# A three-layer CIN on one core: four first-half chunks instead of five ahead of the second layer's weights, and seven shared groups instead of six

## The chip, the core and the metric

The kernel runs on one core of one Trainium2 chip. The metric is the device time of one execution in microseconds; lower is better. Before the change it is 500.84 us, the median of three runs (500.74 to 501.07). The profiled execution has a span of 499.2 us; all times of the profile below are counted from the start of that span.

## The reference

A batch of 1024 samples has 64 fields of 16 values each. Three layers of "compressed interaction" follow one another, and the sums of their outputs give one number for each sample:

```python
x0 = h = x                                   # (1024, 64, 16), float32
for i in range(3):                           # W0, W1, W2: 128 outputs each
    z = einsum('bfe,bge->bfge', x0, h)       # all products of a field of x with a row of h
    y = einsum('oc,bce->boe', W[i], z.reshape(B, -1, E)) + b[i]
    x_i, h = (y[:, :64], y[:, 64:]) if i < 2 else (y, y)
    xs.append(x_i)
pooled = concatenate(xs, axis=1).sum(axis=2)
return pooled @ fc_w.T + fc_b
```

Every weight beyond the first layer's lower half enters the output linearly, so the kernel folds them together. With `fc` for the matching part of `fc_w`:

- `h1` is the first layer's lower half: 64 outputs, each a quadratic form of x.
- V2 is W2 summed over its outputs with `fc`: a 64 x 64 matrix. M is W1's lower half summed with V2: M[f1, f2, g] = sum over o of V2[f1, o] W1[64 + o, f2, g]. So M too gives 64 quadratic forms of x, and the third layer is the sum over g of h1[g] times M's form g, plus small terms.
- V1 and V0 are the upper halves of W1 and W0 summed with `fc`: V1 is linear in x and is added to M's form, V0 is one quadratic form of x.

So each sample needs 128 quadratic forms of x, 64 from W0 and 64 from M, and M has to be computed first, from W2 and W1.

## The kernel before

The batch is cut into 32 chunks of 32 samples, so a chunk has 512 columns (32 samples x 16 values). Of each chunk the products of two fields are made by VectorE: 16 tiles of 128 products x 512 columns, in four instructions of four tiles each (`product(c, j)`, j = 0 to 3, line 166), from two copies of x that are shifted against one another (`xa`, `xb`, 1 MB each). ScalarE puts the 32 squares that fit into the last group (line 171). The squares left over make a 17th, smaller tile (`last_tile`).

TensorE contracts these tiles with `w_all`, whose columns 0 to 63 are W0's, 64 to 127 M's and 128 to 191 W0's again. All is float32, so each matmul is two instructions in the profile. There are three ways to do a chunk:

- As two halves, `half_contract(c, part, j)`, line 237: part 0 is h1 and needs W0 alone, part 1 is M's and needs M. The 512 columns are split over the two halves of the array's columns. `keep_h1` (line 243) saves part 0's result in `hb`.
- Whole, `contract(c, j)`, line 198, 128 outputs at once, with a 17th tile of its own (`contract_last`, line 205).
- Whole, with a shared 17th tile: four chunks' squares lie one below another in one tile, and `contract_shared` (lines 207 to 224) does the four in one go, with V1's and V0's matmuls (`acc` and `y`) of all four chunks. Only chunks from `FIRST` on do this.

M is not there at the start. So the kernel first does part 0 of five chunks, `HEAD = [4, 5, 6, 0, 1]`, called c0 to c4, and puts the work on M between them. In TensorE's order: c0; V2's two sums over W2 (line 307); two groups of c1; V2's transposition (line 324); one more group of c1; M's matmuls (line 336); the rest of c1; c2; c3; three groups of c4. M is written to DRAM (six transfers, lines 357 to 363, onto a square that is extended on two sides) and read back skewed (lines 393 to 406: two transfers, then eight `ms` reads of 256-byte pieces, then `dg` and `w_sq`), and VectorE adds the two orders of fields into `w_all` (line 415). The reads wait for all writes. The last two heads, chunks 0 and 1 (`KEPT`), keep their products, so their part 1 follows as soon as M is there. The other three heads, 4, 5 and 6, have their products made again later, for part 1. The loop over the remaining work goes `order = 2, 3, 4, ..., 31` and makes the products of the chunk two places ahead.

What sets the order: it is written out by hand. Each engine runs its instructions in the order of the program, and a tile of a pool waits until the readers of the tile that had its place are done. There are 12 places for products (`z`), 3 for `xa` and for `xb`, and in PSUM 4 for `acc`, 2 for `y` and 2 for `set`. In the loop `v0x(k)` (line 267) computes V0's form for the pair of chunks 2k and 2k + 1 into a `y` tile, and `x_v0x(k)` (line 270) reads that tile on VectorE; `contract_shared` writes two `y` tiles as well. `factors(c)` (lines 257 and 263) multiplies the two halves of a chunk, and `sums` (line 274) sums them over the 16 values.

The sums of W1 and W0 with `fc` (`weigh`, lines 436 and 437) go to VectorE between the products of the first chunks behind M.

Of the kernel before, what the change touches and what calls it, by code (L numbers as in the profile page):

```python
# [44 lines left out]
N = CB * E  # L45
# [3 lines left out]
NT = NI * NJ  # L49
XR = 128 + NI  # L50
EXT = 96
HEAD = [4, 5, 6, 0, 1]
NF = len(HEAD)
KEPT = HEAD[-2:]
NV = 200
FIRST = 8
SQ = slice(96, 128)


# [1 line left out]
def cin_kernel(ctx, tc, xra, xrb, xh, wh, w0r, w1h, w2t, wx1, wx0, vec, out):  # L61
# [51 lines left out]
    nc.gpsimd.memset(bd, 0.0)  # L113


    xas, xbs, zls, xxs = {}, {}, {}, {}

    def load_xa(c, at=slice(0, NI)):
        if c not in xas or at.start == 0:
# [12 lines left out]
        nc.sync.dma_start(out=xb, in_=xrb[c])  # L132
        xbs[c] = [xb[:, j, :] for j in range(NJ)]

    c0, c1, c2, c3, c4 = HEAD
    xb0 = z_tile("xb0")
    w0t = z_tile("w0t")
    w2s = [flat_tile(f"w2_{k}") for k in range(2)]
# [9 lines left out]
    load_chunk(c1)  # L148
    for k in range(2):
        nc.sync.dma_start(out=w2s[k], in_=w2t[k])  # L150
    load_chunk(c2)
    nc.sync.dma_start(out=w1s, in_=w1h)


    acc = const_tile("acc", [128, 2, NCH // 2, CB])
# [3 lines left out]
    def new_acc(c, n=N):  # L159
        accs[c] = ps.tile([128, n], F32, tag="acc", name=f"acc_{c}", bufs=4)  # L160

    def product(c, j, pieces=1):
        zs[c, j] = z_tile(f"z_{c}_{j}")
        n = NI // pieces
        for i in range(0, NI, n):
            nc.vector.tensor_tensor(  # L166
                zs[c, j][:, i : i + n, :], xas[c][:, i : i + n, :],
                xbs[c][j].unsqueeze(1).to_broadcast([128, n, N]), ALU.mult,
            )
        if j == NJ - 1:  # L170
            nc.scalar.activation(zs[c, j][SQ, 0, :], xas[c][SQ, 0, :], AF.Square)  # L171

# [4 lines left out]
    def last_tile(c):  # L177

        if c < FIRST:
            squares(c)  # L180
            nc.scalar.copy(zls[c][64:128], xas[c][64:128, 0, :])  # L181
        else:
            if c % 4 == 0:
                zls[c // 4] = xp.tile([128, N], F32, tag="zl", name=f"sq_{c}", bufs=4)
            at = 32 * (c % 4)
            nc.scalar.activation(zls[c // 4][at : at + 32], xas[c][0:32, 0, :], AF.Square)  # L186
# [8 lines left out]
    def contract(c, j):  # L195
        for i in range(NI):
            t = j * NI + i
            nc.tensor.matmul(  # L198
                accs[c], w_all[:, t, w_cols(c)], zs[c, j][:, i, :],
                start=(t == 0 and (c < FIRST or c % 4 < 2)),  # L200
                stop=(t == NT - 1 and c >= FIRST and c % 4 >= 2),
            )

    def contract_last(c):
        nc.tensor.matmul(accs[c], w_all[:, NT, 0:128], zls[c], start=False, stop=True)  # L205

    def contract_shared(first):

        for r in range(4):
            c, at = first + r, slice(32 * r, 32 * r + 32)  # L210
            nc.tensor.matmul(  # L211
                accs[c], w_sq[at, w_cols(c)], zls[first // 4][at], start=(r >= 2), stop=(r < 2),
                tile_position=(32 * r, 0),
            )
# [35 lines left out]
    def factors(c):  # L250

        uu = uu_tile(c // 2)[halves[c % 2], 0, :]
        if c in HEAD:
            for n in range(2):
                at = halves[n]
                nc.vector.tensor_tensor(  # L256
                    uu[:, n * H2 : (n + 1) * H2], accs[c][at], hb[at, HEAD.index(c), :], ALU.mult
                )
            return
        h = halves[c % 2 if c >= FIRST else 0]  # L260
# [25 lines left out]

    new_acc(c0, H2)
    squares(c0)
    for j in range(NJ):
        product(c0, j, 2 if j == 0 else 1)  # L290
        if j == NJ - 1:
            nc.vector.memset(w0s[j][SQ, 0, 1, :], 0.0)
        h1_weights(j)
# [21 lines left out]
    new_acc(c1, H2)  # L315
    for j in range(NJ - 1):
        product(c1, j)
    for j in range(2):
        half_contract(c1, 0, j)
    pt = ps.tile([128, F // 4, 4], F32, tag="acc", name="pt", bufs=4)  # L320
    v2q = v2r.rearrange("p n (s o) -> p (n s) o", o=F)
    for q in range(F // 4):
# [1 line left out]
            nc.tensor.matmul(pt[to, q, :], v2q[:, q, :], pick, start=True, stop=True)  # L324
    nc.scalar.copy(v2t, pt.rearrange("p q k -> p (q k)"))
    product(c1, NJ - 1)
    half_contract(c1, 0, 2)
    load_chunk(c4)


    m_sb = z_tile("m_sb")
# [8 lines left out]
    for m in range(NI):  # L340
        nc.scalar.copy(m_sb[:, m, :], pms[m])  # L341

    for j in range(3, NJ + 1):
        half_contract(c1, 0, j)


# [27 lines left out]
    def head(c):  # L374
        new_acc(c, H2)
        for j in range(NJ):
            product(c, j)
        for j in range(NJ + 1):
            half_contract(c, 0, j)
        keep_h1(c)  # L380

    head(c2)

# [12 lines left out]
        )  # L396
    for i in range(NI):
        for half in range(2):
            queue = nc.scalar if half and i < 2 else nc.sync
            queue.dma_start(  # L400
                out=ms[halves[half], 1].rearrange("p (j i) g -> p j i g", i=NI)[:, :, i, :],
                in_=skewed(i, 16 * half + 4, [[4 * F, NJ], [1, F]]),
            )
# [11 lines left out]
    nc.vector.tensor_tensor(w_all[:, 0:NT, 64:128], ms[:, 0], ms[:, 1], ALU.add)  # L415
    nc.vector.tensor_copy(w_all[SQ, (NJ - 1) * NI, 64:128], dg[SQ])
    nc.vector.tensor_copy(w_all[0:32, NT, 64:128], w_sq[0:32, 64:128])
    product(c4, NJ - 1)
    load_chunk(2)
    w1x = flat_tile("w1x")  # L420
    nc.sync.dma_start(out=w1x, in_=wx1)
    new_acc(c3, H2)
    for j in range(NJ):
        half_contract(c3, 1, j)
    for j in range(NJ - 1, NJ + 1):
        half_contract(c4, 0, j)
    keep_h1(c4)
    new_acc(c4, H2)
    for j in range(NJ):
        half_contract(c4, 1, j)  # L430

    def weigh(w, fc, out):

# [3 lines left out]
        nc.vector.tensor_reduce(out, w, AX.X, ALU.add)  # L437


    last_tile(2)  # L440
    for j in range(NJ):
        product(2, j)
    v1h = const_tile("v1h", [128, 32])
    weigh(w1x, fcr[:, 64:128], v1h)
    for to in halves:
# [24 lines left out]
    nc.scalar.activation(cst, pc, AF.Identity, bias=fcb, scale=float(E))  # L470


    last_tile(3)
    for j in range(NJ):
        product(3, j)
    v0h = const_tile("v0h", [128, 32])
    weigh(w0x, fcr[:, 0:64], v0h)
    for to in halves:
# [17 lines left out]
        nc.scalar.dma_start(out=outs[:, pairs, :], in_=res[:, pairs, :])  # L496


    order = list(range(2, NCH))
    first, last = slice(0, NP - 1), slice(NP - 1, NP)  # L500
    for s, c in enumerate(order):
        k, shared = c // 2, c >= FIRST
# [6 lines left out]
        if not shared or c % 4 < 2:  # L509
            new_acc(c, H2 if c in HEAD else N)  # L510
        for j in range(NJ):
            if j == 2:
                if s == 0:
                    for n in KEPT:
                        half_contract(n, 1, NJ)
                if s == 1:
                    v0x(0)
                if c % 2 and not shared:
                    v0x(k)
                if s == len(order) - 1:  # L520
                    pool(first, 1)
                    pool(first, 0)
            if c in HEAD:
                half_contract(c, 1, j)
            else:
                contract(c, j)
        if c in HEAD:
# [23 lines left out]
        if c % 2 and not shared:  # L551
            x_v0x(k)
        elif s and c % 2 == 0:
            sums(k - 1)
    sums(NP - 1, parts=slice(1, 2))
    sums(NP - 1, slice(0, 64), slice(0, 1))
    pool(last, 1)
# [76 lines left out]
```

## Time and profile before

| engine | busy us | share of the span |
|---|---|---|
| TensorE matmuls (PE) | 483.8 | 97% |
| TensorE weight loads (PEld, beside the matmuls) | 222.6 | 45% |
| VectorE (DVE) | 381.8 | 76% |
| ScalarE (ACT) | 92.5 | 19% |

The transfers move 82.8 MB, 166 GB/s over the span, but in the first 40 us, while weights and first chunks arrive, some 420 GB/s. A line of the profile names the engine, the line of the kernel and the tiles (output <- inputs); a bracket at its end is the time in which the engine stood still before it, and what ended that. In a timeline the two numbers at the front are the start and the length in us. Of a wait for several things the profile names the last one by its reckoning.

Four moments of the span matter: the first matmul at 8.44 us, M's writes issued at 33.56, M's columns in `w_all` complete at 53.4, and the loop's first matmul at 72.57.

### The profile page before, as it was taken

What the parts mean: (1) busy time and instruction counts of PE and PEld (TensorE: products, weight loads), DVE (VectorE), ACT (ScalarE), POOL (GpSimd) and SP (SyncE); (2) the same over time, 40 slices, a digit from 0 to 9 for tenths busy, and PEclk for the clock granted to TensorE, in tenths of its full rate; (3) what the DMA queues carried; (4) which work ended last, traced back from release to release, by engine and by line L of the source; (5) the groups of instructions that cost most, each with busy time, mean ns of one, the idle gap of its engine ahead of it and who ended that gap; (6) DMA issues with size and microseconds to landing.
All of it is one profiled execution on the core that took longest, in us unless ns stands there. A gap on an engine that the chain in (4) does not pass through costs nothing.

```text
span 499.2 us, 4338 instructions
## 1 busy us (share of the span) xinstructions
PE 483.8 (97%) x1814; PEld 222.6 (45%) x1814; DVE 381.8 (76%) x233; ACT 92.5 (19%) x159; POOL 1.4 (0%) x14
## 2 busy tenths in 40 slices
PE   3899999999999999999999999999999999999996
PEld 1455654456444344443444434443444434444432
DVE  4999699988999889898777686776877777770302
ACT  1243033122111121312011121111111121010001
POOL 1000000000000000000000000000000000000000
PEclk9999999999999999999999999999999999999999
DMA  8997895353454443446144442333444430000000
GB/s 327 425 419 226 338 421 208 116 230 129 181 235 175 170 174 162 177 175 256 66 169 169 168 168 113 118 136 138 168 169 168 167 131 39 0 0 0 2 0 0
DMA packets 14787, 82.80 MB, mean 166 GB/s; under 512 B 3788, under 2 KB 4460, under 8 KB 5232
## 3 DMA queue, kind: packets, MB, share of 16 engines
q1 hardware_dynamic: 13644, 81.24, 41.5%
q10 hardware_dynamic: 1124, 1.29, 0.9%
q8 instruction: 14, 0.23, 0.2%
q14 instruction: 5, 0.04, 0.0%
HBM read 80.88 MB, written 1.64 MB: 165 GB/s over the span
## 4 chain that ended last, share of the span: by engine, by line
PE 91%; DMA 5%; ACT 1%; ACTq 0%; SPq 0%; DVE 0%; issue 0%
PE acc L198 75%; PE acc L237 11%; DMA w1s<-in_w1h 4%; PE acc L219 2%; DMA xb<-in_xrb 1%; PE acc L211 1%; PE y L267 1%; PE acc L205 1%; PE pm L336 0%; PE po L489 0%; ACT zl L175 0%; ACT zl L181 0%; ACT m_sb L341 0%; ACT xx L190 0%; ACTq L360 0%
## 5 line engine op out<-in xcount | busy, mean ns | idle before, releaser
L198 PE MATMUL acc<-z,w_all 128*128 128x512 f32 x864 | 374.1, 593 | 0.0
L166 DVE TENSOR_TENSOR z<-xa,xb 128x2048 f32<-128x2048 f32 (+1 forms) x141 | 314.9, 2270 | 49.9 <-PE acc L198 39.7
L198 PEld LDWEIGHTS acc<-z,w_all 128*128 128x128 f32 x864 | 163.3, 190 | 208.3 <-issue 207.8
L237 PE MATMUL acc<-z,w_all 128*64 128x256 f32 x640 | 74.7, 389 | 10.4 <-DVE w_all L282 8.4
L171 ACT ACTIVATE z<-xa 32x512 f32<-32x512 f32 x35 | 21.9, 625 | 323.5 <-DVE z L166 320.7
L263 DVE SCALAR_TENSOR_TENSOR uu<-acc,vs,q 64x512 f32<-64x512 f32 x27 | 20.2, 750 | 62.4 <-ACT q L262 62.3
L237 PEld LDWEIGHTS acc<-z,w_all 128*64 128x64 f32 x640 | 45.8, 140 | 39.1 <-DVE w_all L282 9.9
L274 DVE TENSOR_REDUCE acc<-uu 128x64 f32<-128x1024 f32 (+2 forms) x18 | 20.2, 1125 | 0.3
L190 ACT COPY xx<-xa 64x512 f32<-64x512 f32 x32 | 19.6, 613 | 0.4
L262 ACT COPY q<-acc 64x512 f32<-64x512 f32 x27 | 15.7, 580 | 19.3 <-PE y L224 12.9
L186 ACT ACTIVATE sq<-xa 32x512 f32<-32x512 f32 x24 | 15.1, 628 | 0.6
L270 DVE SCALAR_TENSOR_TENSOR uu<-y,cx,xx 128x512 f32<-128x512 f32 x16 | 11.4, 745 | 0.3
L224 PE MATMUL y<-xx,bd 64*64 64x512 f32 x48 | 11.6, 602 | 0.0
L219 PE MATMUL acc<-xx,v1w 64*64 64x512 f32 x48 | 11.6, 602 | 0.0
L211 PE MATMUL acc<-sq,w_sq 32*128 32x512 f32 x48 | 6.8, 640 | 0.0
L175 ACT ACTIVATE zl<-xa 64x512 f32<-64x512 f32 x11 | 6.8, 623 | 0.1
L219 PEld LDWEIGHTS acc<-xx,v1w 64*64 64x64 f32 x48 | 2.8, 132 | 7.9 <-issue 7.9
L237 PE MATMUL acc<-zl,w_all 64*64 64x256 f32 (+1 forms) x40 | 6.1, 393 | 0.0
L243 ACT ACTIVATE hb<-acc,vs 128x256 f32<-128x256 f32 x5 | 2.4, 474 | 20.0 <-PE acc L237 20.0
L495 ACT ACTIVATE res<-po,cst 2x480 f32<-2x480 f32 (+1 forms) x2 | 0.9, 464 | 24.0 <-PE po L489 24.0
L181 ACT COPY zl<-xa 64x512 f32<-64x512 f32 x8 | 4.9, 616 | 0.1
L256 DVE TENSOR_TENSOR uu<-acc,hb 64x256 f32<-64x256 f32 x10 | 4.2, 421 | 0.2
(52 smaller groups left out, 52.0 us busy)
## 6 DMA issues: line engine op xcount, KB each, us to landing
xa<-in_xra SPq DMA_DIRECT2D x34, 1024.0 KB, 4.8
xb<-in_xrb SPq DMA_DIRECT2D x34, 1024.0 KB, 7.0
w<-in_w2t SPq DMA_DIRECT2D x2, 1024.0 KB, 13.5
xa<-in_xra SPq DMA_DIRECT2D x2, 512.0 KB, 4.1
w1s<-in_w1h SPq DMA_DIRECT2D x1, 1024.0 KB, 20.3
w1x<-in_wx SPq DMA_DIRECT2D x1, 1024.0 KB, 8.7
w0x<-in_wx SPq DMA_DIRECT2D x1, 1024.0 KB, 10.3
xb<-in_xrb SPq DMA_DIRECT2D x1, 768.0 KB, 7.0
```

Source lines behind the costliest of these rows:

```text
L166: nc.vector.tensor_tensor(zs[c, j][:, i : i + n, :], xas[c][:, i : i + n, :], xbs[c][j].unsqueeze(1).to_broadcast([128, n, N]), ALU.mult,)
L171: nc.scalar.activation(zs[c, j][SQ, 0, :], xas[c][SQ, 0, :], AF.Square)
L186: nc.scalar.activation(zls[c // 4][at : at + 32], xas[c][0:32, 0, :], AF.Square)
L190: nc.scalar.copy(xxs[c // 2][to], xas[c][to, 0, :])
L198: nc.tensor.matmul(accs[c], w_all[:, t, w_cols(c)], zs[c, j][:, i, :], start=(t == 0 and (c < FIRST or c % 4 < 2)), stop=(t == NT - 1 and ...
L211: nc.tensor.matmul(accs[c], w_sq[at, w_cols(c)], zls[first // 4][at], start=(r >= 2), stop=(r < 2), tile_position=(32 * r, 0),)
L219: nc.tensor.matmul(accs[c][q], v1w[rows], xxs[k][rows], start=False, stop=(c % 4 < 2), skip_group_check=True,)
L224: nc.tensor.matmul(ys[k][rows], bd[rows, rows], xxs[k][rows], start=True, stop=True)
L237: nc.tensor.matmul(accs[c][halves[n]], w_all[rows, t, cols], z[rows, n * H2 : (n + 1) * H2], start=(t == 0), stop=(t == NT),)
L262: nc.scalar.copy(q[h], accs[c][64 - h.start : 128 - h.start])
L263: nc.vector.scalar_tensor_tensor(uu, accs[c][h], bh1[h], q[h], ALU.add, ALU.mult)
L274: nc.vector.tensor_reduce(acc[rows, parts, k, :], uus[k][rows, parts].rearrange("p k (b e) -> p k b e", e=E), AX.X, ALU.add,)
```

## The change

The change does one head fewer, and gives the chunks 4 to 7 to the cheaper shared way: the heads are the chunks 2, 3, 0 and 1, `FIRST` is 4, and the loop goes 4, 5, 6, 7, 2, 3, 8, ..., 31. With it go a new order of the first part and smaller edits:

- Twelve matmuls of zeros (`pw`) at the start, so that TensorE is active before its first data come.
- `w1s` (W1's half for M) is loaded ahead of chunk c2; the first chunk's last weight sum comes ahead of its last product.
- V2's transposition and M's matmuls each come one group of c1 earlier.
- The chunk `FIRST` = 4 is loaded ahead of M's writes, in the place where c4 was loaded, and nothing is loaded beside M's reads. One of M's eight skewed reads goes from SP's queue to ACT's, and `keep_h1(c2)` comes behind the reads.
- The sum that makes M's columns is cut in two, so that the first four tiles are ready sooner, and comes behind the first product of chunk 4. `w1x` takes the place of `ms`.
- In the loop `contract_last` falls away, and the places of `factors`, `v0x` and `sums` follow the new order.

```diff
-HEAD = [4, 5, 6, 0, 1]
+HEAD = [2, 3, 0, 1]
-FIRST = 8
+FIRST = 4
...
+    pw = ps.tile([128, 128], F32, tag="y", name="pw")
+    for k in range(12):
+        nc.tensor.matmul(pw, bd, bd, start=True, stop=True)
...
+    nc.sync.dma_start(out=w1s, in_=w1h)
     load_chunk(c2)
-    nc.sync.dma_start(out=w1s, in_=w1h)
...
+    h1_weights(2)
+    nc.vector.memset(w0s[3][SQ, 0, 1, :], 0.0)
+    h1_weights(3)
+    product(c0, 3)
...
-    for j in range(2):
-        half_contract(c1, 0, j)
+    half_contract(c1, 0, 0)
...
     product(c1, NJ - 1)
-    half_contract(c1, 0, 2)
-    load_chunk(c4)
+    half_contract(c1, 0, 1)
+    load_chunk(FIRST)
...
-    for j in range(3, NJ + 1):
+    for j in range(2, NJ + 1):
         half_contract(c1, 0, j)
...
-            queue = nc.scalar if half and i < 2 else nc.sync
+            queue = nc.scalar if half and i < NI - 1 else nc.sync
...
+    keep_h1(c2)
     head(c3)
-    new_acc(c4, H2)
-    for j in range(NJ - 1):
-        product(c4, j)
-        half_contract(c4, 0, j)
-    nc.vector.tensor_tensor(w_all[:, 0:NT, 64:128], ms[:, 0], ms[:, 1], ALU.add)
+    keep_h1(c3)
+    last_tile(FIRST)
+    product(FIRST, 0)
+    for at in (slice(0, NI), slice(NI, NT)):
+        nc.vector.tensor_tensor(w_all[:, at, 64:128], ms[:, 0, at], ms[:, 1, at], ALU.add)
...
-    product(c4, NJ - 1)
-    load_chunk(2)
-    w1x = flat_tile("w1x")
+    for j in range(1, NJ):
+        product(FIRST, j)
+    w1x = set_tile("w1x")
...
+    for c in KEPT:
+        new_acc(c, H2)
+        for j in range(NJ):
+            half_contract(c, 1, j)
...
-    load_chunk(3)
+    load_chunk(FIRST + 1)
...
-    order = list(range(2, NCH))
+    order = [4, 5, 6, 7, 2, 3] + list(range(8, NCH))
...
-        elif not shared:
-            contract_last(c)
         elif c % 4 == 1:
             for n in (1, 2):
                 new_acc(c + n)
             contract_shared(c - 1)
...
-        elif not shared or c % 4 in (0, 3):
+        elif head or c % 4 in (0, 3):
             factors(order[s - 1])
+            if order[s - 1] % 2:
+                sums(order[s - 1] // 2)
         elif c % 4 == 2:
             factors(c - 2)
             factors(c - 1)
             x_v0x(k - 1)
             x_v0x(k)
+            sums(k - 1)
         if s == 1:
             x_v0x(0)
             sums(0)
-        if c % 2 and not shared:
+        if head and c % 2:
             x_v0x(k)
```

More of the change, by code (lines that the diff above doesn't have):

```diff
@@ L113, in cin_kernel @@
     nc.gpsimd.memset(bd, 0.0)
-    xas, xbs, zls, xxs = {}, {}, {}, {}
+    pw = ps.tile([128, 128], F32, tag="y", name="pw")
+    for k in range(12):
+        nc.tensor.matmul(pw, bd, bd, start=True, stop=True)
+    xas, xbs, zls, xxs, sqs = {}, {}, {}, {}, {}
     def load_xa(c, at=slice(0, NI)):
@@ L133, in load_chunk @@
         xbs[c] = [xb[:, j, :] for j in range(NJ)]
-    c0, c1, c2, c3, c4 = HEAD
+    c0, c1, c2, c3 = HEAD
     xb0 = z_tile("xb0")
@@ L160, in new_acc, with product @@
         accs[c] = ps.tile([128, n], F32, tag="acc", name=f"acc_{c}", bufs=4)
[L162 to L169, printed above, removed]
+    def product(c, j, first=0, last=NI):
+        if first == 0:
+            zs[c, j] = z_tile(f"z_{c}_{j}")
+        at = slice(first, last)
+        nc.vector.tensor_tensor(
+            zs[c, j][:, at, :], xas[c][:, at, :],
+            xbs[c][j].unsqueeze(1).to_broadcast([128, last - first, N]), ALU.mult,
+        )
         if j == NJ - 1:
@@ L183, in last_tile @@
             if c % 4 == 0:
-                zls[c // 4] = xp.tile([128, N], F32, tag="zl", name=f"sq_{c}", bufs=4)
+                sqs[c // 4] = xp.tile([128, N], F32, tag="zl", name=f"sq_{c}", bufs=4)
             at = 32 * (c % 4)
-            nc.scalar.activation(zls[c // 4][at : at + 32], xas[c][0:32, 0, :], AF.Square)
+            nc.scalar.activation(sqs[c // 4][at : at + 32], xas[c][0:32, 0, :], AF.Square)
         if c % 2 == 0:
@@ L199, in contract @@
                 accs[c], w_all[:, t, w_cols(c)], zs[c, j][:, i, :],
-                start=(t == 0 and (c < FIRST or c % 4 < 2)),
-                stop=(t == NT - 1 and c >= FIRST and c % 4 >= 2),
-            )
-    def contract_last(c):
-        nc.tensor.matmul(accs[c], w_all[:, NT, 0:128], zls[c], start=False, stop=True)
+                start=(t == 0 and c % 4 < 2), stop=(t == NT - 1 and c % 4 >= 2),
+            )
     def contract_shared(first):
@@ L211, in contract_shared @@
             nc.tensor.matmul(
-                accs[c], w_sq[at, w_cols(c)], zls[first // 4][at], start=(r >= 2), stop=(r < 2),
+                accs[c], w_sq[at, w_cols(c)], sqs[first // 4][at], start=(r >= 2), stop=(r < 2),
                 tile_position=(32 * r, 0),
@@ L259, in factors @@
             return
-        h = halves[c % 2 if c >= FIRST else 0]
+        h = halves[c % 2]
         q = sp.tile([128, N], F32, tag="q", name=f"q_{c}")
@@ L288, in cin_kernel @@
     squares(c0)
[L289 to L293, printed above, removed]
+    product(c0, 0, 0, 2)
+    product(c0, 0, 2, 4)
+    h1_weights(0)
+    product(c0, 1)
+    h1_weights(1)
+    product(c0, 2)
+    h1_weights(2)
+    nc.vector.memset(w0s[3][SQ, 0, 1, :], 0.0)
+    h1_weights(3)
+    product(c0, 3)
     nc.vector.tensor_copy(w_all[0:32, NT, 0:64], w0ds[0:32])
@@ L379, in head @@
             half_contract(c, 0, j)
-        keep_h1(c)
     head(c2)
@@ L406, in cin_kernel @@
     nc.sync.dma_start(out=w_sq[:, 64:128], in_=m_ap(0, 0, [[0, 4], [row + F, 32], [1, F]]))
+    keep_h1(c2)
     head(c3)
-    new_acc(c4, H2)
-    for j in range(NJ - 1):
-        product(c4, j)
-        half_contract(c4, 0, j)
-    nc.vector.tensor_tensor(w_all[:, 0:NT, 64:128], ms[:, 0], ms[:, 1], ALU.add)
+    keep_h1(c3)
[3 more added lines that the diff above has]
+        nc.vector.tensor_tensor(w_all[:, at, 64:128], ms[:, 0, at], ms[:, 1, at], ALU.add)
     nc.vector.tensor_copy(w_all[SQ, (NJ - 1) * NI, 64:128], dg[SQ])
     nc.vector.tensor_copy(w_all[0:32, NT, 64:128], w_sq[0:32, 64:128])
-    product(c4, NJ - 1)
-    load_chunk(2)
-    w1x = flat_tile("w1x")
+    for j in range(1, NJ):
+        product(FIRST, j)
+    w1x = set_tile("w1x")
     nc.sync.dma_start(out=w1x, in_=wx1)
[L422 to L430, printed above, removed]
+    for c in KEPT:
+        new_acc(c, H2)
+        for j in range(NJ):
+            half_contract(c, 1, j)
     def weigh(w, fc, out):
@@ L437, in weigh @@
         nc.vector.tensor_reduce(out, w, AX.X, ALU.add)
-    last_tile(2)
-    for j in range(NJ):
-        product(2, j)
     v1h = const_tile("v1h", [128, 32])
@@ L470, in cin_kernel @@
     nc.scalar.activation(cst, pc, AF.Identity, bias=fcb, scale=float(E))
-    last_tile(3)
+    last_tile(FIRST + 1)
     for j in range(NJ):
-        product(3, j)
+        product(FIRST + 1, j)
     v0h = const_tile("v0h", [128, 32])
@@ L496, in finish @@
         nc.scalar.dma_start(out=outs[:, pairs, :], in_=res[:, pairs, :])
-    order = list(range(2, NCH))
+    order = [4, 5, 6, 7, 2, 3] + list(range(8, NCH))
     first, last = slice(0, NP - 1), slice(NP - 1, NP)
     for s, c in enumerate(order):
-        k, shared = c // 2, c >= FIRST
+        k, head = c // 2, c in HEAD
         if s + 2 < len(order):
@@ L508, in cin_kernel @@
                 product(ahead, j)
-        if not shared or c % 4 < 2:
-            new_acc(c, H2 if c in HEAD else N)
+        if head or c % 4 < 2:
+            new_acc(c, H2 if head else N)
         for j in range(NJ):
@@ L522, in cin_kernel @@
                     pool(first, 0)
-            if c in HEAD:
+            if head:
                 half_contract(c, 1, j)
@@ L526, in cin_kernel @@
                 contract(c, j)
-        if c in HEAD:
+        if head:
             half_contract(c, 1, NJ)
-        elif not shared:
-            contract_last(c)
         elif c % 4 == 1:
@@ L550, in cin_kernel @@
             sums(0)
-        if c % 2 and not shared:
+        if head and c % 2:
             x_v0x(k)
-        elif s and c % 2 == 0:
-            sums(k - 1)
     sums(NP - 1, parts=slice(1, 2))
```

## The prediction

> **What bounds the kernel now.** I read the page first: busy times, then the chain that ended last.
>
> ```profile
> PE 483.8 (97%) x1814; PEld 222.6 (45%) x1814; DVE 381.8 (76%) x233; ACT 92.5 (19%) x159; POOL 1.4 (0%) x14
> ...
> PE 91%; DMA 5%; ACT 1%; ACTq 0%; SPq 0%; DVE 0%; issue 0%
> ```
>
> TensorE carries the end: 15.4 of 499.2 us are not its. Less TensorE work shortens the run, and every new TensorE wait lengthens it by its full length. So I laid out TensorE's own timeline.
>
> ```profile
> 40.50 1.95 PE L237 MATMUL acc<-z,w_all 128*64 128x256 f32 x16 [0.77 <-ACT z L171]
> ...
> 50.59 14.03 PE L237 MATMUL acc<-z,w_all 128*64 128x256 f32 x128
> 64.56 0.65 PE L237 MATMUL acc<-zl,w_all 64*64 64x256 f32 x4
> 65.14 7.13 PE L237 MATMUL acc<-z,w_all 128*64 128x256 f32 x64
> ...
> 72.57 7.13 PE L198 MATMUL acc<-z,w_all 128*128 128x512 f32 x16
> 79.64 1.08 PE L237 MATMUL acc<-zl,w_all 128*64 128x256 f32 x8
> 80.65 7.13 PE L198 MATMUL acc<-z,w_all 128*128 128x512 f32 x16
> ```
>
> From 40.50 on there is no bracket: TensorE never waits. One half of a chunk (64 of its 128 outputs; 64 instructions in the view) takes 6.98 us, with its last tile about 7.6. Chunk 2 starts at 72.57, chunk 8 at 143.81 (later in the same view), and all behind it takes 499.2 - 143.81 = 355.4 us in both kernels.
>
> Next, VectorE, which makes M's columns and all products:
>
> ```profile
> 51.81 1.23 DVE L415 TENSOR_TENSOR w_all<-ms 128x1024 f32<-128x1024 f32 x1 [1.04 <-DMA dg<-md]
> 53.06 0.19 DVE L416 COPY w_all<-dg 32x64 f32<-32x64 f32 x1
> 53.29 0.18 DVE L417 COPY w_all<-w_sq 32x64 f32<-32x64 f32 x1
> 53.40 2.27 DVE L166 TENSOR_TENSOR z<-xa,xb 128x2048 f32<-128x2048 f32 x1
> 58.73 8.89 DVE L166 TENSOR_TENSOR z<-xa,xb 128x2048 f32<-128x2048 f32 x4 [3.06 <-DMA xb<-in_xrb]
> 67.54 2.28 DVE L436 TENSOR_TENSOR w1x<-w1x,vs 128x2048 f32<-128x2048 f32 x1
> ```
>
> M's columns are complete at 53.4; TensorE asks for them at about 55.8 (three groups of 1.73 us behind 50.59). That slack of 2.4 us is bought by the third head. Last, what M waits for: the DMA queue's issues, and stretches of 2 us with DMA share and GB/s as last columns.
>
> ```profile
> 33.56 0.53 SPq L357 DMA_DIRECT2D md<-m_sb  x1
> 43.88 0.65 SPq L393 DMA_DIRECT2D ms<-md  x1
> 44.58 5.32 SPq L400 DMA_DIRECT2D ms<-md  x6
> ...
> 38.00:40.00 2.00, 1.74 (x18) 0.86 (x12) 2.00 (x2) 1.96 (x5) 0.00 (x0) 1.00 1.01 426
> 40.00:42.00 2.00, 1.50 (x14) 1.06 (x16) 2.00 (x2) 0.45 (x1) 0.00 (x0) 1.00 0.85 347
> 42.00:44.00 2.00, 2.00 (x20) 0.95 (x16) 2.00 (x1) 0.47 (x1) 0.00 (x0) 1.00 0.08 32
> 48.00:50.00 2.00, 2.00 (x20) 1.12 (x16) 2.00 (x2) 0.00 (x0) 0.00 (x0) 1.00 1.20 186
> ```
>
> M's writes are issued at 33.56 and land by 43.8, and until 42 the transfers run at about 420 GB/s: the writes stand in a line of bytes, behind chunk loads. The reads go from 43.88 to 51.7 in small pieces, with the DMA engines full (1.20).
>
> [...] M's writes on ACT's queue, issued at 33.57, show their first packets only about 4 us later, when the line in front is through. [...] The kernel's pools take 4 (acc) + 2 (y) + 2 (set)[...]. [...] two weight loads take 0.43 us from 8.93 to 12.74, and 0.22 us after 13.17.
>
> **The change, part by part.**
>
> *Start.* The 12 `pw` matmuls lie before 8.4 us, where TensorE has no data. The cold clock they remove costs nothing now: the second group starts at 12.26 and the third at 14.80, both on VectorE's `w_all`, though the groups before were done. Moving the last weight sum ahead of the last product moves the last group of the first chunk from 17.7 to about 18.15, but V2's second half still starts when its weights land, at 21.4. Zero.
>
> *V2 and M inside the second chunk, `w1s` ahead of chunk c2.* One group fewer lies ahead of V2, and M's matmuls no longer wait for `w1s` (0.30): M's writes are issued about 2.2 us earlier (31.4). But before they can land, the same bytes must move as now (four chunks, W2, W1, chunk FIRST, M), and that line is full until 42. So they land at about 43.7. Gain: 0 to 0.3. Chunk c2 now lands after `w1s`, at about 29.9, where VectorE wants it at 26.5. This delay of 3 us is hidden, as shown next.
>
> *M's reads.* One of eight skewed reads goes from SP to ACT. SP's fifth and sixth anyway stand until 47.79 and 48.95, when the first two reads have landed. Worth 0 to 0.3. On ACT's queue `keep_h1(c2)` and c3's square are behind the reads: they end near 48.3, and c3's last two groups then end near 50.6. I take the first add on M at A = 51.6 (51.81 now; bounds 51.0 and 52.6, should a landing slip).
>
> *No third head.* TensorE is through its heads at 50.6 and M's first quarter is in at A + 0.47 = 52.1 (0.42 for a 256-column sum, as L282, and 0.05 to wake): **a new wait of 1.5 us**. Splitting the add shortens it by 0.9.
>
> *TensorE from A*: 0.47, kept halves 2 x 6.98, `pcx` and `pc` 0.38: chunk 4 starts at A + 14.81. It takes 15.05 (as chunk 2 now, 72.57 to 87.62). Chunk 5 takes 6.87 + 0.86 (`v0x(0)`) + 6.87 = 14.60: A + 44.46. Then the shared tiles, whose last y matmuls start 1.99 later (171.37 to 173.36 now): A + 46.45.
>
> *A wait that the text of the diff does not show.* Chunk 5 is now second in the order and also ends a pair of a shared group. So `v0x(0)`, y of chunks 4 and 5, and y of chunks 6 and 7 want three y tiles in a row with two banks. The third must wait until `x_v0x(0)` has read the first, and on VectorE that stands behind all products of chunk 7. VectorE from A: adds 1.63, three products 6.63 (2.21 each), W1's sums 5.42 (67.54 to 72.96), chunk 5 8.81, W0's sums 5.48, chunk 6 8.93, the kept factors 1.78, chunk 7 8.89, `x_v0x` 0.73: A + 48.30. TensorE would be there at A + 46.45, so it **waits 1.9 us**, with chunk 6's matmuls queued behind it. Now the first shared group comes at 171 us, when y's readers are long done.
>
> *From there*: y at A + 48.35, chunk 6 0.96 later, chunks 6 and 7 27.56 (143.81 to 171.37 now), head chunk 2 7.49, head chunk 3 with `v0x` 8.65, then 355.4: the end is at A + 448.4. With A = 51.6 it is 500.0, against 499.2.
>
> *The same as a sum of TensorE's work.* One chunk's first half less (-7.6) and chunks 2 to 7 behind the heads at 76.3 instead of 71.2 (+5.1: four of them whole with shared last tiles, two as second halves, where now three were halves): -2.5. The new waits give +3.4; some 0.1 goes back at the old waits (0.30 and 0.77, part of which moves to other places). Net +0.8. The median is 1.64 above the profiled span: 500.0 + 1.64 = **501.6**.
>
> Not a bound: products for later chunks have buffers in time (chunk 5's are free after c3's first group, A + 9; needed at A + 13.7), chunk 5 lands near 63, needed at 65, and `w1x`, in `ms`'s place, near 57.6, needed at 60.
>
> **Rivals.** *Slower still*: the reads slip by a microsecond, for ACT is busier around them, or a 16 KB instruction fetch (one at 48.05 now, taking 1.4 us) falls badly. A = 52.6, time 502.6. For it: everything from here moves one to one with A. Against it: the reads' traffic is unchanged. *Faster*: the y wait is hidden because VectorE is earlier, or TensorE later, than I have it. Then A + 446.5, 498.1 + 1.64 = 499.7. For it: 1.9 us is a difference of two sums near 47. Against it: both start at A and are sums of measured rows. *M early*: the writes, issued 2.2 us earlier, really land 1.5 us earlier. A = 50.1, and TensorE goes from head to second half without a wait: 500.1. Against it: the full line until 42.
>
> **How the numbers follow.** The forecast has 0.55, slower still 0.20, faster 0.13, M early 0.12. 0.2% is 1.0 us: the bounds are 499.8 and 501.8. The forecast is close under the upper one, so of its 0.55 I count 0.35 as the same and 0.20 as slower. M early: 0.10 same, 0.02 faster. Sums: faster 0.15, same 0.45, slower 0.40. The range goes from the faster rival, 499.7, to just over the slower one, 502.8.
>
> **What would show it.** TensorE's timeline should have a wait of 1 to 2 us on VectorE's `w_all` near 52, a second one of about 2 us at L224's (y) matmuls near 98 to 100 with `x_v0x` as releaser, and chunk 8 at about 144.6. M's writes should be issued near 31.4 and the reads start near 43.7. It is wrong if the reads start before 42.5, if the y matmuls go through without a wait, or if some other releaser stands before TensorE between 20 and 145 us.

## The result, and the profile after

The changed kernel takes 502.63 us (median; 502.33 to 502.94), the kernel before beside it 500.96 (500.74 to 501.07): the ratio is 1.0033, with a 95% interval of 1.0020 to 1.0046. The change makes the kernel slower by 1.67 us, where 0.6 to 0.8 was forecast. In the two profiled executions the span goes from 499.2 to 500.5 us.

From the page of the changed kernel, the busy times, the chain that ended last, and the group of the y matmuls:

```profile
PE 485.2 (97%) x1748; PEld 223.3 (45%) x1748; DVE 373.7 (75%) x229; ACT 89.7 (18%) x154; POOL 1.4 (0%) x14
...
PE 87%; DVE 5%; DMA 5%; SPq 1%; issue 1%; ACT 1%; ACTq 0%; DVEq 0%
...
L225 PE MATMUL y<-xx,bd 64*64 64x512 f32 x56 | 13.8, 604 | 0.8 <-DVE uu L271 0.8
```

TensorE executes 66 instructions fewer, although 24 were added at the start. Its busy time rises all the same, because the 24 take 4.8 us in which it had nothing else to do. What counts is the second line: TensorE's share of the chain falls from 91% to 87%, and VectorE's goes from nothing to 5%. The chain now runs through a wait for VectorE. The third line has a releaser, `uu`, before a y matmul, which the kernel before didn't have.

TensorE's timeline of the changed kernel (start, length, engine, line, what is written and read, count; in brackets the idle time before, and what ended it):

```profile
48.52 1.95 PE L238 MATMUL acc<-z,w_all 128*64 128x256 f32 x16 [0.97 <-ACT z L176]
50.40 0.65 PE L238 MATMUL acc<-zl,w_all 64*64 64x256 f32 x4
52.57 14.03 PE L238 MATMUL acc<-z,w_all 128*64 128x256 f32 x128 [1.52 <-DVE w_all L421]
66.91 7.13 PE L203 MATMUL acc<-z,w_all 128*128 128x512 f32 x16
...
98.63 1.02 PE L220 MATMUL acc<-xx,v1w 64*64 64x512 f32 x4
100.40 1.08 PE L225 MATMUL y<-xx,bd 64*64 64x512 f32 x4 [0.75 <-DVE uu L271]
101.41 27.73 PE L203 MATMUL acc<-z,w_all 128*128 128x512 f32 x64
```

Two waits stand where no bracket was before: 1.52 us for M's columns at 52.57, and one for y at 100.40. The second shows only 0.75, because two V1 matmuls of the second pair run meanwhile. Its real size is read between two starts: from the second halves (52.57) to chunk 6 (101.41) it is 48.84 us, and in the runs below that have no y wait and a full clock it is 47.02 to 47.03. The y wait costs 1.81. Chunk 8 starts at 145.11 where it started at 143.81, so the whole 1.3 us of the span is lost ahead of it.

VectorE's timeline, and under it the issues of SP's DMA queue, in the changed kernel:

```profile
52.00 1.29 DVE L421 TENSOR_TENSOR w_all<-ms 128x256 f32<-128x256 f32 x2 [2.04 <-DMA dg<-md]
...
90.67 8.90 DVE L171 TENSOR_TENSOR z<-xa,xb 128x2048 f32<-128x2048 f32 x4
99.60 0.75 DVE L271 SCALAR_TENSOR_TENSOR uu<-y,cx,xx 128x512 f32<-128x512 f32 x1
```

```profile
31.43 0.53 SPq L364 DMA_DIRECT2D md<-m_sb  x1
...
43.84 0.65 SPq L399 DMA_DIRECT2D ms<-md  x1
44.53 5.52 SPq L406 DMA_DIRECT2D ms<-md  x5
50.09 0.61 SPq L411 DMA_DIRECT2D dg<-md  x1
```

VectorE stands 2.04 us before it can add M's columns at 52.00: the reads end the wait, not VectorE. At 99.60 `x_v0x(0)`, the reader that frees the first y tile, comes straight behind chunk 7's four products, and 0.8 us later the third y goes through. M's writes are issued at 31.43, 2.1 us earlier than before, and yet the reads start at 43.84, as they did before (43.88).

### The profile page after: what moved, and what is told of

It reads as the page before. It is cut to its first block, busy times and chain, and to the rows that moved or that the text cites. A ratio compares the mean times of both kernels' runs of the same rounds, so it can differ in the third digit from the quotient of the medians.

```text
span 500.5 us, 4185 instructions
## 1 busy us (share of the span) xinstructions
PE 485.2 (97%) x1748; PEld 223.3 (45%) x1748; DVE 373.7 (75%) x229; ACT 89.7 (18%) x154; POOL 1.4 (0%) x14
## 3 DMA queue, kind: packets, MB, share of 16 engines
HBM read 78.79 MB, written 1.64 MB: 161 GB/s over the span
## 4 chain that ended last, share of the span: by engine, by line
PE 87%; DVE 5%; DMA 5%; SPq 1%; issue 1%; ACT 1%; ACTq 0%; DVEq 0%
PE acc L203 75%; PE acc L238 7%; DVE z L171 4%; DMA md<-m_sb 2%; PE acc L220 2%; DMA xb<-in_xrb 1%; PE acc L212 1%; DMA ms<-md 1%; PE po L490 0%; DMA dg<-md 0%; PE pm L343 0%; PE pv L313 0%; PE pt L331 0%; PE y L225 0%; SPq L406 0%
## 5 line engine op out<-in xcount | busy, mean ns | idle before, releaser
L203 PE MATMUL acc<-z,w_all 128*128 128x512 f32 x896 | 387.6, 593 | 0.0
L171 DVE TENSOR_TENSOR z<-xa,xb 128x2048 f32<-128x2048 f32 (+1 forms) x137 | 306.8, 2271 | 58.4 <-PE acc L203 47.7
L203 PEld LDWEIGHTS acc<-z,w_all 128*128 128x128 f32 x896 | 169.3, 190 | 216.3 <-issue 215.9
L238 PE MATMUL acc<-z,w_all 128*64 128x256 f32 x512 | 58.5, 382 | 7.9 <-DVE w_all L283 3.5
L238 PEld LDWEIGHTS acc<-z,w_all 128*64 128x64 f32 x512 | 37.2, 137 | 29.5 <-DVE w_all L283 4.6
L191 ACT ACTIVATE sq<-xa 32x512 f32<-32x512 f32 x28 | 17.6, 628 | 0.6
L225 PE MATMUL y<-xx,bd 64*64 64x512 f32 x56 | 13.8, 604 | 0.8 <-DVE uu L271 0.8
L118 PE MATMUL pw<-bd 128*128 128x128 f32 x24 | 4.8, 390 | 2.3 <-POOL bd L113 2.3
L118 PEld LDWEIGHTS pw<-bd 128*128 128x128 f32 x24 | 4.7, 301 | 2.3 <-POOL bd L113 2.3
L212 PEld LDWEIGHTS acc<-sq,w_sq 32*128 32x128 f32 x56 | 2.2, 182 | 5.3 <-issue 5.3
```

Source lines behind the costliest of these rows:

```text
L171: nc.vector.tensor_tensor(zs[c, j][:, at, :], xas[c][:, at, :], xbs[c][j].unsqueeze(1).to_broadcast([128, last - first, N]), ALU.mult,)
L191: nc.scalar.activation(sqs[c // 4][at : at + 32], xas[c][0:32, 0, :], AF.Square)
L203: nc.tensor.matmul(accs[c], w_all[:, t, w_cols(c)], zs[c, j][:, i, :], start=(t == 0 and c % 4 < 2), stop=(t == NT - 1 and c % 4 >= 2),)
L212: nc.tensor.matmul(accs[c], w_sq[at, w_cols(c)], sqs[first // 4][at], start=(r >= 2), stop=(r < 2), tile_position=(32 * r, 0),)
L238: nc.tensor.matmul(accs[c][halves[n]], w_all[rows, t, cols], z[rows, n * H2 : (n + 1) * H2], start=(t == 0), stop=(t == NT),)
```

## The experiments

The kernel before, run beside each group, took 500.96 to 501.02 us. All runs start from the changed kernel, and the edits are against it unless something else is said.

**A place of its own for the disputed y tile.** The tile of pair 0 goes into the pool tag whose two places are free by then:

```diff
-        ys[k] = ps.tile([128, N], F32, tag="y", name=f"y_{k}")
+        ys[k] = ps.tile([128, N], F32, tag="y" if k else "set", name=f"y_{k}")
```

> V0's form of the pair 0, 1 gets a place in PSUM of its own kind (tag set), so chunk 4's shared matmuls no longer wait for x_v0x(0). My theory (the wait of 1.9 us before the third y tile costs its full length): 502.6 - 1.9 = 500.7 us, no wait at the y matmuls near 98 us, chunk 8 at about 143.2 us. Rival (VectorE is simply late, and TensorE meets the same lag at a later wait): no wait at y, but a new one of about 2 us on products or factors before 145 us, and still about 502.5 us.

Measured: 501.93 us, but scattered from 500.73 to 504.5 over 22 runs; ratio 1.0021 (1.0012 to 1.0030). The y wait is gone from the trace. The profiled execution took 502.92 us, and shows why not all of it was gained. TensorE's timeline, then stretches of 2 us with, in the last three columns, the granted clock, the DMA share and GB/s:

```profile
53.32 15.72 PE L238 MATMUL acc<-z,w_all 128*64 128x256 f32 x128 [2.03 <-DVE w_all L421]
```

```profile
54.00:56.00 2.00, 2.00 (x14) 1.51 (x12) 1.93 (x4) 0.00 (x0) 0.00 (x0) 0.60 0.27 66
56.00:58.00 2.00, 2.00 (x13) 1.39 (x11) 2.00 (x2) 0.00 (x0) 0.00 (x0) 0.55 1.02 426
58.00:60.00 2.00, 2.00 (x22) 1.57 (x20) 2.00 (x2) 0.00 (x0) 0.00 (x0) 1.00 0.98 414
```

The same 128 instructions take 15.72 us here and 14.03 in the changed kernel. The clock is at half for 3.41 us behind the wait for M, and so 1.7 us of work is lost. The spans of the 22 runs fall into two groups, 498.8 to 499.9 us in 13 and 500.8 to 501.7 in 9, which fits a loss of that size in some executions; the course of the clock is on record for the profiled one alone. In five runs about 1 us more lies outside the span (2.7 to 2.9 from span to time, where 1.8 is usual), so not all of the scatter is the clock's. This run alone does not price the y wait.

**The changed kernel again**, to see whether it too loses the clock, and how its times scatter.

> The changed kernel again, beside the next three. In the run with the y tile of its own kind the granted clock was half for 3.4 us behind a wait of 2.0 us for M; the changed kernel's own profile had a wait of 1.5 us and no such drop. If the drop belongs to the wait for M and not to that edit, some executions of the changed kernel should have it too: times from 502.3 up to about 504.5. If it doesn't, all lie within 0.6 us of 502.6.

Measured: 502.77 us (502.43 to 502.93), ratio 1.0034 (1.0022 to 1.0047). TensorE's timeline of this execution, and VectorE's `x_v0x(0)`:

```profile
53.05 15.72 PE L238 MATMUL acc<-z,w_all 128*64 128x256 f32 x128 [1.78 <-DVE w_all L421]
```

```profile
100.07 0.75 DVE L271 SCALAR_TENSOR_TENSOR uu<-y,cx,xx 128x512 f32<-128x512 f32 x1
```

This execution did lose the clock, 1.69 us of it, and its time is still that of the others. The reason is in the second line. VectorE reads the first y at 100.07 whatever TensorE does; TensorE arrives late, finds hardly a wait, and starts chunk 6 at 101.89, which is 48.84 us behind 53.05, just as in the execution with the full clock. The y wait, which VectorE sets, swallows what TensorE loses ahead of it.

**The y tile, and zeros to keep the clock up.** The first edit, and between the heads and M's matmuls six matmuls on zeros that nobody reads:

```diff
+    pf = ps.tile([128, 128], F32, tag="y", name="pf")
+    for k in range(6):
+        nc.tensor.matmul(pf, bd, bd, start=True, stop=True)
     for c in KEPT:
```

> The y tile of its own kind, and six matmuls of zeros (about 1.3 us at full clock) between the heads and M's matmuls, so that TensorE is active while it waits. My theory: the wait for M stays as long as it is, but the clock no longer falls to half behind it: about 500.8 us, the fastest of the 22 executions without the filling (500.7), and a spread of under 1 us. Rival (the spread comes from when M's reads land): as without the filling, 500.7 to 504.5, median near 501.9.

Measured: 500.82 us (500.62 to 501.37), ratio 0.9998 (0.9990 to 1.0006). TensorE's timeline:

```profile
51.06 1.60 PE L433 MATMUL pf<-bd 128*128 128x128 f32 x12
52.94 14.03 PE L238 MATMUL acc<-z,w_all 128*64 128x256 f32 x128 [0.27 <-DVE w_all L421]
...
99.96 27.73 PE L203 MATMUL acc<-z,w_all 128*128 128x512 f32 x64
```

The mean granted clock of this execution is 1.00, the 128 instructions take 14.03 us again, and all 13 spans lie between 498.8 and 499.6. Against the changed kernel's 502.63 to 502.77, removing the y wait is worth 1.81 to 1.95 us. The wait for M is not shorter: the first add on M comes at 52.45, later than the 52.00 of the changed kernel's profiled execution, and TensorE spends the wait on zeros.

**The order on VectorE instead of the place.** The y tile stays in its two places, and `v0x(0)` and `x_v0x(0)` move ahead of chunk 7's products; the six matmuls stay.

```diff
-                if s == 1:
-                    v0x(0)
...
+            v0x(0)
...
+            x_v0x(0)
...
-            x_v0x(0)
```

The two plus lines stand at the end of the first loop step (`s == 0`).

> The changed kernel with the tile of y left in its two places and the order on VectorE altered instead: v0x and the product that frees the first place go ahead of chunk 7's products; six matmuls on zeros before M's products keep the clock up as in the run that had them. Theory: it is the order on VectorE that makes the wait for y, not the number of places as such, so the time is as with y in a place of its own and the same filling: 500.6 to 501.1 us, with no wait ahead of the second pair's y. Rival: the second place is what is missing whatever the order, and the wait comes back in some other form: 502.4 to 502.9 us.

Measured: 500.98 us (500.65 to 501.25), ratio 1.0000 (0.9992 to 1.0008). VectorE's timeline:

```profile
91.13 0.75 DVE L271 SCALAR_TENSOR_TENSOR uu<-y,cx,xx 128x512 f32<-128x512 f32 x1
91.80 8.88 DVE L171 TENSOR_TENSOR z<-xa,xb 128x2048 f32<-128x2048 f32 x4
```

The reader now stands at 91.13, ahead of chunk 7's products, and TensorE goes from 52.95 to chunk 6 at 99.97 in 47.02 us. So two places are enough; the wait comes from the reader's place in VectorE's order.

**M first.** Chunk 4's load moves behind M's reads, and its first product behind M's adds. y stays as in the changed kernel.

```diff
-    load_chunk(FIRST)
...
     nc.sync.dma_start(out=w_sq[:, 64:128], in_=m_ap(0, 0, [[0, 4], [row + F, 32], [1, F]]))
+    load_chunk(FIRST)
...
-    product(FIRST, 0)
     for at in (slice(0, NI), slice(NI, NT)):
...
-    for j in range(1, NJ):
+    for j in range(NJ):
```

> Chunk 4 is loaded behind M's reads instead of ahead of M's writes, and M's columns are summed ahead of chunk 4's first product. My theory: the writes then land 5 us earlier (about 38.8 instead of 43.7, 2 MB less in the line), the reads by about 47, and TensorE's wait before M goes from 1.5 to about 0.4 us. But chunk 4 now lands near 53.3, its products end at about 62.2 instead of 60.3, and everything up to x_v0x(0) follows on VectorE, so the y wait grows to about 5 us: about 504.5 us, slower than the changed kernel although M comes earlier. Rival (the wait for M is what costs, the y wait is slack that any earlier start takes up): 502.6 - 1.5 = 501.1 us or less.

Measured: 509.56 us (509.13 to 509.83), ratio 1.0168 (1.0155 to 1.0181), 5 us more than expected. TensorE, VectorE, and two stretches around the y wait:

```profile
103.21 1.97 PE L225 MATMUL y<-xx,bd 64*64 64x512 f32 x4 [5.37 <-DVE uu L271]
```

```profile
102.40 0.75 DVE L271 SCALAR_TENSOR_TENSOR uu<-y,cx,xx 128x512 f32<-128x512 f32 x1
```

```profile
102.00:104.00 2.00, 0.79 (x2) 0.29 (x4) 1.93 (x3) 1.56 (x3) 0.00 (x0) 0.50 0.01 4
...
106.00:108.00 2.00, 2.00 (x4) 0.85 (x3) 2.00 (x2) 0.00 (x0) 0.00 (x0) 0.50 0.99 401
```

M's part went the expected way, if not as far: the reads start at 40.01, not 43.84 (the writes were to land at 38.8), and the second halves begin at 50.75 without a wait. But VectorE stands 3.94 us for chunk 4's load (its products start at 54.23), so `x_v0x(0)` comes at 102.40 and not 99.60. TensorE, which is earlier by the 1.8 us it no longer waits, stands 5.37; counted from start to start, as above, this y wait is 6.4 us, not the 5 expected. The clock is at half for 6.83 us, from 101.35 to 108.18. TensorE still waits in the first 1.9 of them, and the rest costs it 2.4 us: the y matmuls take 1.97 and not 1.08, and chunks 6 and 7 take 29.24 and not 27.73. Together chunk 8 starts at 150.31, 5.2 us later than in the changed kernel. Taking away the first wait alone, at the price of a later chunk 4, made the second one dearer.

**Both waits away**: M first, and the y tile in a place of its own.

> Both edits together: the y tile of its own kind, and chunk 4 loaded behind M's reads. My theory: both waits go, and VectorE's lag of 2 us finds no one waiting: 502.6 - 1.9 - 1.2 = 499.5 us, faster than both kernels. Rival (the gains overlap, one wait covering the other): no better than the better one of the two alone, about 500.7.

Measured: 499.79 us (499.57 to 500.62), ratio 0.9977 (0.9967 to 0.9986). It beats both kernels. TensorE's timeline:

```profile
50.88 14.03 PE L238 MATMUL acc<-z,w_all 128*64 128x256 f32 x128
...
97.91 27.73 PE L203 MATMUL acc<-z,w_all 128*128 128x512 f32 x64
...
141.61 27.73 PE L203 MATMUL acc<-z,w_all 128*128 128x512 f32 x64
```

From 50.88 on no bracket is left. From the start of V2's sums to chunk 8 it is 121.13 us (20.48 to 141.61), where the kernel before has 123.62 (20.19 to 143.81). The difference, 2.49 us, is what the change saves of TensorE's work. Not all of it reaches the time: V2 starts 0.29 later, and in this execution the span ends 2.9 us behind the last transfer's issue (495.04 to 497.9), where before it was 2.1 (497.09 to 499.2).

**The start without its zeros.** The twelve `pw` matmuls left out.

> The changed kernel without the twelve matmuls of zeros at the start. My theory: nothing, within 0.3 us of 502.6, because TensorE waits for VectorE's weights in the first chunk and then for W2 whether its clock is up or not; its first groups run at half speed again until about 13 us. Rival (the first chunk ends later with a cold clock and all of the chain to M with it): 0.5 to 1.5 us slower.

Measured: 502.87 us (502.3 to 503.45), ratio 1.0035 (1.0022 to 1.0048), the same as with them within the scatter of its four runs (502.30, 502.44, 503.30 and 503.45). In the profiled one, the slowest, the first chunk does end 0.9 us later than in the changed kernel, but not for the clock: TensorE's first groups wait for VectorE there too, and VectorE waits 1.40 us for a load of x.

**Both waits away, and the old order of V2 and M.** c2 is loaded ahead of `w1s` again, and `pt` and `pm` come one group later, as in the kernel before.

```diff
-    nc.sync.dma_start(out=w1s, in_=w1h)
     load_chunk(c2)
+    nc.sync.dma_start(out=w1s, in_=w1h)
...
+    half_contract(c1, 0, 1)
     pt = ps.tile([128, F // 4, 4], F32, tag="acc", name="pt", bufs=4)
...
-    half_contract(c1, 0, 1)
+    half_contract(c1, 0, 2)
...
-    for j in range(2, NJ + 1):
+    for j in range(3, NJ + 1):
```

> Both waits taken away as before (499.8), and chunk c2 ahead of w1s again, with V2's transposition and M's matmuls where the kernel before had them. My theory: M's writes are issued 2 us later (33.5) but land when they did, since the line of bytes sets that; VectorE no longer waits 3.8 us for c2, so c3's last products and with them the end of the heads come 0.5 to 1 us earlier: 498.9 to 499.3. Rival (M's matmuls in the second chunk were worth their place): about 2 us slower, 501.8.

Measured: 501.13 us (500.63 to 502.43), ratio 1.0006 (0.9999 to 1.0012). The expectation was wrong by about 2 us; the rival was nearer. TensorE's timeline, then ScalarE's:

```profile
94.93 2.42 PE L212 MATMUL acc<-sq,w_sq 32*128 32x512 f32 x8
```

```profile
95.02 0.63 ACT L191 ACTIVATE sq<-xa 32x512 f32<-32x512 f32 x1
```

M's writes are issued at 33.42 and the reads start at 42.07. That is 8.65 us later, and with both waits away it was 8.63 (31.38 to 40.01). With chunk 4 out of the way the landing follows the issue, so 2.04 us of issue cost 2.06 us of M. Chunk 4's load stands behind the reads, its products start at 56.91 and not 55.34, and everything on VectorE moves with them. ScalarE makes chunk 7's squares only at 95.02, behind chunk 6's products, and the shared matmuls that need them take 2.42 us and not 1.14. Here the new order of `w1s`, V2 and M, taken as one, is worth 1.3 us (501.13 - 499.79).

**The same, with less on ScalarE ahead of the heads.** The tile of c3 is made behind the head of c2, and c2's squares, made twice, only once:

```diff
-    squares(c2)
-    for c in KEPT:
-        last_tile(c)
+    last_tile(c2)
...
     head(c2)
+    last_tile(c3)
```

> The same with ScalarE's squares and copies for the second kept chunk behind the first one's square, and the doubled squares of c2 left out. My theory: c2's last group no longer waits for ScalarE, another 0.3 to 0.8 us: 498.3 to 498.9 us, if M's columns are there by 49.5. Rival (M's columns then end the wait again, near 48.8 to 50): no gain over the run without this edit.

Measured: 500.35 us (499.65 to 500.82), ratio 0.9988 (0.9982 to 0.9995), again 1.5 to 2 us above the expectation. The heads end 0.84 earlier, at 49.76 and not 50.60, but M's columns come only 0.11 earlier: the wait for M grows from 0.26 to 0.98 us, and the shared matmuls still wait (2.70 us). Chunk 8 starts at 143.02, no earlier than without this edit (142.85). The 0.8 us between the two medians is therefore not gained ahead of chunk 8, and what gives it stays open; in the profiled pair the span differs by 0.4, and the stretch behind the last transfer's issue by 0.5 (2.7 and 2.2).

**The ScalarE edit alone**, on the version with both waits away.

> The version with both waits taken away (499.79 us) with one further edit on ScalarE: the head of the third stretch reads its tile of M's convolution only once, and the doubled squares of that stretch are left out; the order of V2, M and chunks 0 to 3 stays. Theory: the first matmuls of the heads wait for VectorE more than for ScalarE, so at most 0.3 us is gained: 499.4 to 499.8 us. Rival: the ScalarE work ahead of the heads sets their start, and then its 1.0 to 1.5 us come off: 498.3 to 498.8 us.

Measured: 499.30 us (498.99 to 500.09), ratio 0.9969 (0.9959 to 0.9979), the fastest of all. But the edit did nothing on TensorE: the second halves start at 50.89 (50.88 without it), chunk 8 at 141.74 (141.61). In the profiled pair the span is 0.5 us shorter (497.4 and 497.9) because less time passes behind the last transfer's issue (2.2 us and 2.9), where the edit has no part. So the 0.5 us is not claimed for it.

**The read back on SP's queue.** What was left open was why M's columns come later than forecast.

```diff
-            queue = nc.scalar if half and i < NI - 1 else nc.sync
+            queue = nc.scalar if half and i < 2 else nc.sync
```

> The changed kernel with one thing undone: the third upper-half read of M's skewed copies is again issued on SP's queue, not ACT's. In the changed kernel the first add on M comes 8.16 and 8.24 us after the start of the reads, in the kernel before 7.93; the end follows that add one to one. Theory: the read on ACT's queue lengthens the reads, so with it back the add comes 7.9 us after the reads' start and the time is 502.1 to 502.4 us. Rival: the length of the reads varies by itself and the queue is worth nothing: 502.5 to 502.9 us, with the add still 8.1 us or more behind the start of the reads. The prediction had held the move to ACT for worth 0 to 0.3 us: then this run is that much slower, up to 503.0 us.

Measured: 502.88 us (502.6 to 503.07), ratio 1.0037 (1.0024 to 1.0049). The first add comes at 52.39, 8.27 us behind the start of the reads (44.12). The theory falls: the read on ACT's queue does not lengthen the reads. 502.88 against 502.63 and 502.77 agrees with the forecast's 0 to 0.3 us in its favour, which these runs do not resolve.

**The order around the reads as before**: the read on SP's queue, and `keep_h1(c2)` ahead of the reads.

> The same, and the saving of the second stretch's result on ScalarE stands ahead of M's reads again, so that the whole order around the reads is that of the kernel before. Theory: as with the read alone, 502.1 to 502.4 us, for that saving does not touch the reads. Rival: ScalarE's instruction delays the reads on its own queue, which start when it is through, and the time is 502.6 to 503.2 us.

Measured: 503.13 us (502.97 to 503.89), ratio 1.0045 (1.0031 to 1.0059). The time is in the rival's range, but the rival's reason is not there. ACT's queue issues its first read at 43.87, beside SP's at 43.84, and the first add comes at 52.66, 8.82 behind. What lengthens the reads is neither of the two edits around them; what the traces show of it stands in the next section.

## Why the prediction was nearly right, point by point

The kernel became slower through two waits, in the places forecast. The time is 1.0 us above the forecast of 501.6, near the upper end of the stated range.

- *TensorE's work, -2.5 us.* Right: 2.49 where both waits are away.
- *The y wait that the diff does not show, 1.9 us.* Right in size, place and cause: 1.81 in the trace, 1.7 to 1.9 in the medians (500.82 and 500.98, each with the zeros, against 502.63 and 502.77). Giving the tile a place and moving its reader each remove it. That the third y tile must wait holds for y's own two places only: `set` had room for it. `x_v0x(0)` ended at 100.35, which is A + 48.35 for a forecast of 48.30, and the y matmuls ran at 100.40, A + 48.40 for 48.35. The difference of two sums near 47 us came out within 0.1 us. Two rows were misread on the way, with little effect: the two head chunks behind chunk 7 were put at 16.14 us (7.49 + 8.65), where such chunks take 15.98 in the kernel before (7.43 + 8.55) and 16.04 in the changed one.
- *A new wait for M, 1.5 us with A = 51.6.* The wait is there, but **A is the term that was mis-sized**. The first add on M came at 52.00 in the profiled execution of the changed kernel, 52.48 in the repeated one and 53.16 without `pw`. The spans are 500.5, 501.0 and 501.7, and A + 448.4 gives 500.4, 500.9 and 501.6. With the read back and with the old order around the reads the spans, 501.1 and 501.3, lie 0.3 and 0.2 above it. So the end does follow A one to one, within 0.3 us, and most of the miss is in A. The wait itself came out at 1.52 for a forecast of 1.5, but partly by luck: the heads ended at 51.05 where 50.6 was forecast, 0.4 late like A. To the median of 502.63 belongs an A of about 52.3 (502.63, less the 1.83 between time and span of the profiled execution, less 448.5). The time is that of the rival *slower still* (A = 52.6, 502.6), to which 0.20 was given and not 0.55. The rest of the miss is small: 0.1 in the sum behind A (TensorE starts 0.57 behind the add, not 0.47), and 1.83 instead of 1.64 from the span to the time.
- *Why A was later.* In the profiled execution the reads started on time (43.84 for 43.7), but they were longer than before. From their start to the first add on M it is 7.93 us in the kernel before, and 8.16 to 8.90 in the eight executions on record that keep chunk 4 ahead of the writes. The prediction had left this length as it was, since the reads' traffic is unchanged. The queues show what it overlooked. SP's last two `ms` reads are issued only when an earlier read has landed, and in the changed kernel that is another read. The lines show, of the kernel before, the first reads with the us from issue to landing in the last column, and SP's last two `ms` reads; then these last two in the changed kernel:

```profile
ms<-md SPq DMA_DIRECT2D x1, 256.0 KB, 3.9
ms<-md ACTq DMA_DIRECT2D x1, 256.0 KB, 5.0
```

```profile
47.79 2.10 SPq L400 DMA_DIRECT2D ms<-md  x2
```

```profile
48.81 1.23 SPq L406 DMA_DIRECT2D ms<-md  x2
```

Before, the first of the two is issued 3.91 us behind the start of the reads, when SP's own first read has landed (3.90), and the second at 5.08, when ACT's first has (5.06). In the changed kernel the first of the two waits for ACT's first read, which lands at 4.96, and goes at 4.97; the second follows at 5.59, and `dg` behind it. By the landings in the traces it is so in all eight executions, those of the last two experiments included: it is issued 0.01 to 0.02 us behind the landing of ACT's first read, 4.97 to 5.72 us behind the start. The first add follows the issue of `dg` by 1.8 to 2.0 us in all of them. Why the changed program lets this read wait for the other landing is open.

A 16 KB instruction fetch, which the prediction had named, goes with the rest of the length, but not in the profiled execution of the changed kernel. There it ends 1.44 us behind the start of the reads, just as their first packets move. In the four executions where it ends by then, or comes only at 4.4 us, the length is 8.16 to 8.27; in the four where it ends later, at 1.52 to 1.86, it is 8.67 to 8.90, and there the last of the sixteen parts of SP's first read lands 1.2 to 1.5 us behind the fifteenth, where it is at most 0.2 in the others. This is a comparison of executions: no run moved the fetch alone.
- *M's writes issued 2.2 us earlier, landing at 43.7 because of the line of bytes.* Right in its numbers (31.43, 43.84). With chunk 4 out of the line the reads start at 40.01, so it was chunk 4's 2 MB, ahead of the writes, that held them. The step said nothing of the case without it: there the landing follows the issue by 8.6 us, and the earlier issue is worth its full length.
- *`pw` at nothing.* Right: 502.87 without, 502.63 and 502.77 with.
- *The read on ACT's queue, 0 to 0.3 us.* It agrees with the runs, which do not resolve it.
- *Not foreseen: the clock.* The prediction counted the two waits at their own length. In some executions the first also loses 1.7 us of clock (128 instructions take 15.72 us and not 14.03, with the clock at half for 3.41). In the changed kernel this costs nothing, for the y wait swallows it; it shows as soon as y is mended.

The change as a whole saves 2.5 us of TensorE's work and pays 3.4 for two waits, counted from start to start (1.6 and 1.8), and 0.4 by a later start of V2 (20.54 for 20.19) and slightly longer heads. That makes the 1.3 us by which chunk 8 starts later.

## What to carry to other kernels

When an order of work is changed, list the live tiles of each small pool in the new order, and for each the reader that frees it and what stands ahead of that reader on its engine. Here that list found a wait of 1.8 us of which the diff shows nothing. Two waits on one path have to be taken away together: the later one, set by another engine, swallows what is gained or lost ahead of it. Against the kernel before the change stood at +1.7 us, with y mended alone at +0.9 (at -0.1 with the zeros), with M mended alone at +8.6, because chunk 4's later load makes VectorE and with it the y wait later, and with both at -1.2. And where a bulk load and a small dependent round trip competed, the issue order decided which of them was waited for: with chunk 4's load ahead, M's reads started at 43.84 us and TensorE stood 1.52 us for M; with the load behind them they started at 40.01, and VectorE stood 3.94 us for chunk 4.

## What was not expected of the hardware

- In four executions a wait for M of 1.78, 1.95, 2.03 and 2.22 us, 2.5 us behind another wait of 0.8 to 1.2, was followed by some 3.4 us at half clock; in two others, with waits of 1.52 and 1.63, it was not. A wait of 5.37 was followed by 6.83 us at half clock, counted from within the wait. The stretches from one change of the granted clock to the next lie on a grid of 3.41 us: 484.69 and 491.52 us at full clock in the kernel before and the changed one, 142 and 144 times 3.413, and 3.41 and 6.83 at half clock in the runs. The earlier wait lies in another step of that grid. In the step ahead of the drop TensorE had stood for 1.76 to 2.22 us of 3.41, in the two executions without a drop for 1.52 and 1.61; elsewhere in the traces a few steps with 1.77 to 1.90 us kept the clock, so no border is read from these numbers.
- With six matmuls on zeros, in a wait that had to be waited anyway, the clock was 1.00 behind it in both profiled executions (54 to 60 us), and the scatter of the spans, with y in a place of its own, went from 2.9 us (498.8 to 501.7) to 0.8 (498.8 to 499.6).
- From the issue of M's writes to DRAM to the issue of the first read that depends on them it is 8.6 us when chunk 4 is not ahead of them, in either order of V2 and M, and 11.7 to 12.5 us in six executions with chunk 4's 2 MB ahead of them (12.41 in the profiled one of the changed kernel).
- The last of a transfer's sixteen parts landed 1.2 to 1.5 us behind the fifteenth where a 16 KB instruction fetch of 0.9 to 1.2 us was still under way when the transfer's first packets moved (four executions of SP's first read), and at most 0.2 behind it where none was (four others).
